# State-space recurrence by channel halves, and other PSUM banks for the input of the last experts

## The chip, the cores and the metric

The kernel runs on one core of one Trainium2 chip. The metric is the device time of a launch in microseconds (us). The core has five engines with a queue each: TensorE (PE in the profile; its weight loads are PEld), VectorE (DVE), ScalarE (ACT), GpSimd (POOL) and SyncE (SP), which here only issues DMAs. Each queue is worked off in order.

## What is computed

The model is a two-layer block on 64 x 32 tokens of width 256, and each sublayer adds its result to `x`. The order is: cross-attention, RWKV and a two-of-eight expert layer (layer 0); then cross-attention with quantised projections, a selective state-space model and a gated expert layer (layer 1). The change lies in the last two. Cut to what matters:

```python
# L1_attn: 512 inner channels, 16 states, over the 32 time steps of each sequence
xz = x @ in_proj_w.T + in_proj_b ; x_main, z = split(xz)
xc = silu(conv(x_main))
B, C, delta = split(xc @ x_proj_w.T + x_proj_b) ; dt = softplus(delta)
A = -exp(A_log)                                   # (512, 16)
h[t] = exp(A * dt[t]) * h[t-1] + dt[t] * B[t] * xc[t]     # for every channel and state
y[t] = sum_over_states(h[t] * C[t]) + D * xc[t]
out = layernorm(y * silu(z) @ out_proj_w.T + out_proj_b + x)
# L1_ffn: all eight experts are computed
g = softmax(2 * rmsnorm(x @ gate_w.T + gate_b)).max()
out = g' * sum_over_e( gelu(x @ w1[e] + b1[e]) @ w2[e] + b2[e] ),  g' = g / (g + 1e-6)
```

Ahead of each sublayer `x` is normalised over its 256 columns.

## The kernel before

The 2048 tokens are cut into four blocks of 512 (`BT`), numbered b = 0 to 3. In channel layout a block is a tile of 128 partitions (channels) by 512 columns (tokens), so the 512 inner channels are four such pieces, c = 0 to 3 (`C = 4`), and the 16 states are `N = 16`. `_stage3` is the quantised attention, `_stage4` the state-space model, `_stage5` the last experts. `layers` calls them interleaved: while attention works on the units of one block, the state-space model runs for the block before, and the experts for the one before that.

Stage 4 has three parts. `ahead(b)` normalises, projects in, convolves, and computes `dt` (its last step is L1077). `gates(v)` makes `zs = silu(z)`. `recur(b, v)` first makes `dtx = dt * xc` (L1096), sets `dt` to a huge value at the first step of each sequence so that the state starts anew (L1098, POOL), and then loops over the states n, and inside over the two halves of the channels, c2 = 0 and 2. A turn for one state and one half consists of

- L1105, POOL: `g = dtx * B`, 128 x 1024
- L1109, ACT: `h = exp(A * dt)` into a PSUM tile of the pool `psh` (tag "h", two banks), once for each of the half's two pieces
- L1110, DVE: the scan over time, in place, and L1111, DVE: `hc = h * C`, once for each piece
- L1116, POOL: `y += hc`, 128 x 1024 (`y` lies in the tile `xc`, by which name the profile knows it).

A recurrence is thus 32 turns and 64 tiles `h`. `B` and `C` of a state reach all partitions by one DMA of 512 KB from DRAM into a tile `bc` (L1102, SP queue), which serves both halves. `bc`, `g` and `hc` have two buffers each, in the last recurrence (b = 3, where memory of the attention has become free) three. After all states L1119 (POOL) multiplies each half of `y` by `zs`. Then come the output projection `outps` (L1131; L1156 in `end` for block 3), also in `psh`, and the layer norm.

Stage 5 has `head(b)` and `block(b)`. `head` normalises x (in the tile `xn5`, one buffer), transposes it through PSUM (`t_ps`, L1210, two tiles) into `xT`, copied by ACT (L1211), and computes the gate's logits (`lg_ps`, L1215) and the gate `gt`. `t_ps` and `lg_ps` lie in `psh` too. `block` streams eight experts' weights by two DMAs of 512 KB each (L1255 and L1256, SP queue), and for each of 32 pieces of the hidden layer does `up` (L1260, PE), a copy with bias (L1262, ACT), after four of them a Gelu (L1264, ACT), and `acc` (L1268, PE). The results are transposed (`rT`, L1281) and written out (L1284). `up` uses the pool `psu` (one bank); blocks 2 and 3 use attention's pool `ps` (two banks) for two of three pieces; `rT` is in `psu` for block 0 and in `ps` after it.

Nobody writes the order on an engine by hand. A planner works through the program with costs of its own: of what is ready on an engine, the earliest in program order goes first; a tile gets a bank or buffer of its tag when an earlier tile has given one back. The queues it makes are then fixed. The program order around the change is the end of `layers`: `s5(0)`, `head(1)`, `ahead(3)`, `recur(2)`, `gates(3)`, `head(2)`, `s5(1)`, `recur(3)`, `head(3)`, `s5(2)`, `s5(3)`, where `s5` is `block`.

Of the kernel before, what the change touches and what calls it, by code (L numbers as in the profile page):

```python
# [8 lines left out]
F32 = mybir.dt.float32  # L9
# [6 lines left out]
P = 128  # L16
# [3 lines left out]
NBLK = 4  # L20
BT = NTOK // NBLK
# [49 lines left out]
def _chan(k, name, j=0):  # L71
    at = CHAN_AT[name] + j
    return k.chan[:, at : at + 1]
# [40 lines left out]
def _norm(k, out, x, mv, rstd, j):  # L114
    k.nc.vector.tensor_scalar(out, x, mv[:, j, 0:1], rstd[:, j : j + 1], ALU.subtract, ALU.mult)
# [862 lines left out]
def _stage4(k, w, wk):  # L978
# [4 lines left out]
    nc, i = k.nc, k.i  # L983
    N, C = 16, 4
# [23 lines left out]
    def ph(shape, name):  # L1008
        return k.psh.tile(shape, F32, name=name, tag="h")
# [77 lines left out]
    def recur(b, v, mem=None):  # L1087
        xs = [k.x[b][:, j, :] for j in range(4)]
        dt, y = v.dt, v.y
        if b == NBLK - 1:  # L1090
            xn = residual(v, xs)
        own, more = (mem, 1) if mem else (wk, 0)
        dtx = wk.tile([P, C, BT], F32, name="dtx", tag="dtx", bufs=1)
        for c2, eng in ((0, nc.vector), (2, nc.gpsimd)):
            yc = y[:, c2 : c2 + 2]
            eng.tensor_tensor(dtx[:, c2 : c2 + 2], yc, dt.unsqueeze(1).to_broadcast([P, 2, BT]), ALU.mult)  # L1096

        nc.gpsimd.memset(dt.rearrange("p (b t) -> p b t", t=T)[:, :, 0:1], 1e20)  # L1098
        bc_rows = v.rows[0 : 2 * N].rearrange("(two n) t -> n two t", two=2)
        for n in range(N):  # L1100
            bc = own.tile([P, 2, BT], F32, name="bc", tag="bc", bufs=2 + more)
            nc.sync.dma_start(bc, bc_rows[n].partition_broadcast(P))  # L1102
            for c2 in range(0, C, 2):
                g = own.tile([P, 2, BT], F32, name="g", tag="g", bufs=2 + more)
                nc.gpsimd.tensor_tensor(g, dtx[:, c2 : c2 + 2], bc[:, 0:1, :].to_broadcast([P, 2, BT]), ALU.mult)  # L1105
                hc = own.tile([P, 2, BT], F32, name="hc", tag="hc", bufs=2 + more)
                for c in range(2):
                    h = ph([P, BT], "h")
                    nc.scalar.activation(h, dt, AF.Exp, scale=A[:, c2 + c, n : n + 1])  # L1109
                    nc.vector.tensor_tensor_scan(h, h, g[:, c, :], 0.0, ALU.mult, ALU.add)  # L1110
                    nc.vector.tensor_tensor(hc[:, c, :], h, bc[:, 1, :], ALU.mult)  # L1111
                if n == 0:

                    for c in range(c2, c2 + 2):
                        nc.scalar.activation(y[:, c, :], y[:, c, :], AF.Copy, scale=_chan(k, "L1_attn_D", c))
                nc.gpsimd.tensor_tensor(y[:, c2 : c2 + 2], y[:, c2 : c2 + 2], hc, ALU.add)  # L1116

        for c2 in range(0, C, 2):
            nc.gpsimd.tensor_tensor(y[:, c2 : c2 + 2], y[:, c2 : c2 + 2], v.zs[:, c2 : c2 + 2], ALU.mult)  # L1119
        if b == NBLK - 1:  # L1120
            for j2 in range(0, 4, 2):
                end(v, xs, xn, j2)
            return
        xn = wk.tile([P, 4, D], F32, name="xe4", tag="hc", bufs=2)
        xn = [xn[:, j, :] for j in range(4)]
        for j in range(4):
            nc.scalar.activation(xn[j], xs[j], AF.Identity, bias=v.off[:, j : j + 1], scale=v.rstd[:, j : j + 1])
            nc.gpsimd.tensor_tensor(xn[j], xn[j], bout, ALU.add)
            ps = ph([P, D], "outps")
            for c in range(C):  # L1130
                nc.tensor.matmul(ps, y[:, c, j * P : (j + 1) * P], wout[:, c, :], start=c == 0, stop=c == C - 1)  # L1131
            nc.vector.tensor_tensor(xn[j], ps, xn[j], ALU.add)
        mv, rstd = _stats(k, xn, "4b")
        for j in range(4):
            _norm(k, xn[j], xn[j], mv, rstd, j)
            nc.gpsimd.tensor_tensor(xn[j], xn[j], gamma, ALU.mult)
            nc.gpsimd.tensor_tensor(xs[j], xs[j], beta, ALU.add)
            nc.gpsimd.tensor_tensor(xs[j], xs[j], xn[j], ALU.add)

    def residual(v, xs):  # L1140


        xn = wk.tile([P, 4, D], F32, name="xr4", tag="xT4", bufs=1)
        for j in range(4):
            _norm(k, xn[:, j, :], xs[j], v.mv, v.rstd, j)
            nc.gpsimd.tensor_tensor(xn[:, j, :], xn[:, j, :], bout, ALU.add)
            nc.gpsimd.tensor_tensor(xs[j], xs[j], beta, ALU.add)
        return xn

    def end(v, xs, xn, j2):  # L1150

        ps = ph([P, 2, D], "outps")
        for j in range(2):
            for c in range(C):
                at = slice((j2 + j) * P, (j2 + j + 1) * P)
                nc.tensor.matmul(ps[:, j, :], v.y[:, c, at], wout[:, c, :], start=c == 0, stop=c == C - 1)  # L1156
        t = xn[:, j2 : j2 + 2, :]
        nc.vector.tensor_tensor(t, ps, t, ALU.add)
        mv, rstd = _stats(k, [t[:, j, :] for j in range(2)], "4e", wk, nc.vector)
        for j in range(2):  # L1160
            x = xs[j2 + j]
            nc.vector.scalar_tensor_tensor(t[:, j, :], t[:, j, :], mv[:, j, 0:1], gamma, ALU.subtract, ALU.mult)
            nc.vector.scalar_tensor_tensor(x, t[:, j, :], rstd[:, j : j + 1], x, ALU.mult, ALU.add)
# [7 lines left out]
def _stage5(k, w, out):  # L1171


    nc, i = k.nc, k.i
    E, H = 8, 4
# [8 lines left out]
    def ps(shape, name, free=False):  # L1184

        return k.ps.tile(shape, F32, name=name, tag="s") if free else k.psu.tile(shape, F32, name=name, tag="u")
# [6 lines left out]

    def head(b, mem):

        v = Ctx()
        xs = v.xs = [k.x[b][:, j, :] for j in range(4)]
        pairs = b == NBLK - 1
        if not pairs:
            mv, rstd = _stats(k, xs, "5")  # L1200
        xT = v.xT = mem.tile([P, 2, BT], F32, name="xT5", tag="xT5")
        for j2 in range(0, 4, 2):
            xn = k.wk5.tile([P, 2, D], F32, name="xn5", tag="xn5", bufs=1)
            t_ps = k.psh.tile([P, 2, 2 * P], F32, name="t_ps", tag="h")
            if pairs:
                mv, rstd = _stats(k, xs[j2 : j2 + 2], "5e", k.wk5, nc.vector)
            for j in range(2):
                _norm(k, xn[:, j, :], xs[j2 + j], mv, rstd, j if pairs else j2 + j)
                for c in range(2):
                    nc.tensor.transpose(t_ps[:, c, j * P : (j + 1) * P], xn[:, j, c * P : (c + 1) * P], k.ident)  # L1210
            nc.scalar.copy(xT[:, :, j2 * P : (j2 + 2) * P], t_ps)  # L1211
        lg_ps = k.psh.tile([P, 4, E], F32, name="lg_ps", tag="h")
        for j in range(4):
            for c in range(2):
                nc.tensor.matmul(lg_ps[:, j, :], xT[:, c, j * P : (j + 1) * P], wg[:, c, :], start=c == 0, stop=c == 1)  # L1215

        def rows(name):
            return k.small.tile([P, 4], F32, name=name, tag=name)

        def over(t):  # L1220
            return t.unsqueeze(2).to_broadcast([P, 4, E])

        lg = k.small.tile([P, 4, E], F32, name="lg", tag="lg", bufs=1)
        sq = k.small.tile([P, 4, E], F32, name="sq", tag="sq", bufs=1)
        nc.vector.tensor_tensor(lg, lg_ps, bg.unsqueeze(1).to_broadcast([P, 4, E]), ALU.add)
        nc.vector.tensor_tensor(sq, lg, lg, ALU.mult)
        ms, mx, gt, gn = rows("ms"), rows("mx"), rows("gt"), rows("gn")
        nc.vector.tensor_reduce(ms, sq, AX.X, ALU.add)
        _rsqrt(k, ms, [(ms, 1.0 / E, F32_EPS)], "5r")
        nc.vector.tensor_tensor(lg, lg, over(ms), ALU.mult)  # L1230
        nc.vector.tensor_tensor(lg, lg, rms.unsqueeze(1).to_broadcast([P, 4, E]), ALU.mult)
        nc.vector.tensor_reduce(mx, lg, AX.X, ALU.max)
        nc.vector.tensor_tensor(lg, lg, over(mx), ALU.subtract)


        nc.scalar.activation(lg, lg, AF.Exp, scale=2.0)
        nc.vector.tensor_reduce(gt, lg, AX.X, ALU.add)
        nc.vector.reciprocal(gt, gt)
        nc.vector.tensor_scalar(gn, gt, 1e-6, None, ALU.add)
        nc.vector.reciprocal(gn, gn)  # L1240
        nc.vector.tensor_tensor(gt, gt, gn, ALU.mult)
        v.gt = gt
        return v
# [213 lines left out]
```

## Time and profile before

| | us |
|---|---|
| median of 3 runs | 2025.51 (2022.17 to 2026.44) |
| profiled execution, time | 2021.33 |
| its span, first to last instruction | 2019.5 |
| POOL busy | 1107.0 (55%) |
| DVE busy | 1279.0 (63%) |
| ACT busy | 997.7 (49%) |
| first and last `h` of the four recurrences (ACT) | 780 to 999, 1102 to 1331, 1427 to 1662, 1715 to 1867 |
| first `up` and end of `acc` of the four expert blocks (PE) | 1109 to 1425, 1436 to 1727, 1717 to 1870, 1900 to 2013 |
| last attention softmax (ACT L893) | 1542 |

A row of a timeline has the start in us, the duration, the engine, the line, the operation, what it writes and reads, and in brackets how long the engine was idle before it and whose end released it. A row of the table by stretches has the length of the stretch and then the busy time of each engine, the granted clock of TensorE, the mean busy share of the DMA engines and what they moved in GB/s. Parts of one execution fit together to a hundredth of a microsecond; executions differ by more, as the range of the three runs shows.

### The profile page before, as it was taken

Reading aid. Unit: us, or ns where it says so; the run is one execution under the profiler, and the core shown is the slowest. Engines: PE = TensorE matmul, PEld = TensorE weight load, DVE = VectorE, ACT = ScalarE, POOL = GpSimd, SP = SyncE. Lnnn points to the kernel's source line nnn. Section 1 sums busy time; section 2 is a strip of 40 time slices with the busy share of each in tenths; the row PEclk is TensorE's granted clock in tenths of the full one; section 3 lists DMA queues with packets and bytes.
Section 4 is the critical chain, followed back from the end, with each engine's and each line's share of the span. In section 5 each row is a group of like instructions: output and inputs, shape, how many; then the busy total and the mean of one; then the engine's idle time right before and its main releaser. Section 6 shows DMA issues by size and latency. Waiting matters only on the chain. (4 is left out here: it accounts for less than half of the span.)

```text
span 2019.5 us, 20188 instructions
## 1 busy us (share of the span) xinstructions
PE 1563.2 (77%) x6323; PEld 805.4 (40%) x6323; DVE 1279.0 (63%) x2207; ACT 997.7 (49%) x2171; POOL 1107.0 (55%) x1369
## 2 busy tenths in 40 slices
PE   4775956849988978766778778779888575898798
PEld 3333523525645533433444334334443223333443
DVE  4578576376385267989854788763687593777300
ACT  3453453122554446445537567548466472676232
POOL 5444665423134225777853677763477777899100
PEclk9676877868998989767787889789888797898799
DMA  6755324020100202212201223202122130443021
GB/s 227 232 166 158 117 82 136 27 90 1 37 6 22 63 1 59 63 53 63 73 11 49 63 63 102 76 21 91 53 63 79 51 106 3 112 117 102 32 83 42
DMA packets 88379, 151.26 MB, mean 75 GB/s; under 512 B 7740, under 2 KB 52300, under 8 KB 86224
## 3 DMA queue, kind: packets, MB, share of 16 engines
q1 hardware_dynamic: 85428, 148.75, 24.2%
q10 hardware_dynamic: 2844, 1.22, 0.3%
q8 instruction: 50, 0.82, 0.2%
q14 instruction: 57, 0.47, 0.1%
HBM read 139.03 MB, written 10.92 MB: 74 GB/s over the span
## 5 line engine op out<-in xcount | busy, mean ns | idle before, releaser
L1105 POOL TENSOR_TENSOR g<-dtx,bc 128x1024 f32<-128x1024 f32 x128 | 301.9, 2362 | 126.3 <-DVE h L1110 89.0
L1110 DVE TENSOR_TENSOR_SCAN h<-h,g 128x512 f32<-128x512 f32 x256 | 307.5, 1218 | 62.3 <-ACT h L1109 59.4
L1116 POOL TENSOR_TENSOR xc<-xc,hc 128x1024 f32<-128x1024 f32 x128 | 303.6, 2374 | 23.9 <-DVE hc L1111 18.3
L1260 PE MATMUL up<-xT,w 128*128 128x512 f32 x512 | 274.4, 656 | 22.1 <-ACT hid L1262 21.7
L1268 PE MATMUL acc<-hid,w 128*128 128x512 f32 x512 | 266.5, 646 | 27.8 <-ACT hid L1264 27.8
L1109 ACT ACTIVATE h<-dt,A 128x512 f32<-128x512 f32 x256 | 173.6, 692 | 116.7 <-DVE hc L1111 116.0
L1111 DVE TENSOR_TENSOR hc<-h,bc 128x512 f32<-128x512 f32 x256 | 169.9, 679 | 3.9 <-DVE h L1110 0.4
L893 ACT ACTIVATE p<-sc,nm 128x256 f32<-128x256 f32 x256 | 117.7, 472 | 109.0 <-DVE nm L889 98.1
L1268 PEld LDWEIGHTS acc<-hid,w 128*128 128x128 f32 x512 | 101.8, 208 | 151.5 <-issue 108.4
L630 PE MATMUL weps<-we,xT 128*128 128x512 f32 x256 | 143.2, 687 | 17.5 <-DVE x L632 14.4
L1260 PEld LDWEIGHTS up<-xT,w 128*128 128x128 f32 x512 | 99.6, 207 | 134.6 <-issue 94.4
L1262 ACT ACTIVATE hid<-up,chan 128x512 f32<-128x512 f32 x128 | 86.5, 683 | 104.6 <-PE up L1260 104.4
L882 PE MATMUL sc<-kT,qm 32*128 32x256 f32 x512 | 115.4, 447 | 6.4 <-ACT p L893 2.4
L911 PE MATMUL pt_ps<-ident,p 128*128 128x128 f32 x512 | 90.3, 309 | 28.1 <-ACT p L893 28.0
L887 DVE TENSOR_REDUCE nm<-sc 128x2 f32<-128x512 f32 x128 | 84.1, 683 | 32.6 <-PE sc L882 31.6
L913 ACT COPY pt<-pt_ps 128x512 f32<-128x512 f32 x128 | 73.1, 587 | 46.5 <-PE pt_ps L911 37.7
L911 PEld LDWEIGHTS pt_ps<-ident,p 128*128 128x128 f32 x512 | 63.6, 155 | 69.0 <-ACT p L893 44.3
L247 POOL TENSOR_TENSOR cT<-cT,scb 128x2056 f32<-128x2056 f32 x16 | 74.4, 4648 | 27.4 <-PE sc L258 10.5
L530 POOL TENSOR_TENSOR kk<-kk 128x512 f32<-128x512 f32 x32 | 34.2, 1074 | 94.8 <-ACT kk L529 94.8
L919 PE MATMUL oT_ps<-pt,v 128*32 128x128 f32 x1024 | 68.4, 299 | 22.2 <-ACT pt L913 21.6
L882 PEld LDWEIGHTS sc<-kT,qm 32*128 32x128 f32 x512 | 67.5, 205 | 44.9 <-issue 17.8
L630 PEld LDWEIGHTS weps<-we,xT 128*128 128x128 f32 x256 | 50.6, 215 | 70.0 <-issue 51.9
(407 smaller groups left out, 3068.2 us busy)
## 6 DMA issues: line engine op xcount, KB each, us to landing
bc<-rows SPq DMA_DIRECT2D x64, 512.0 KB
w<-in_L_ffn_w_dram SPq DMA_DIRECT2D x64, 512.0 KB
cT<-in_ctxT_dram SPq DMA_DIRECT2D x16, 1028.0 KB
cq<-cq SPq DMA_DIRECT2D x32, 514.0 KB
cn<-in_ctx_dram SPq DMA_DIRECT2D x64, 256.0 KB
scb<-scales SPq DMA_DIRECT2D x16, 514.0 KB
kb<-steps SPq DMA_DIRECT2D x16, 514.0 KB
x<-in_x_dram SPq DMA_DIRECT2D x4, 512.0 KB
```

Of the source, the lines that this page charges most:

```text
L630: nc.tensor.matmul(ps, xT[:, c, r], we[:, c, e : e + 2, :], start=c == 0, stop=c == 1)
L882: nc.tensor.matmul(sc[h][:, f, :], qm[r, e + f].rearrange("p l n g -> p (l n g)"), kTs[e][r, f, :], start=True, stop=True,)
L893: nc.scalar.activation(w_[:, f, h - h0, :], sc[h][:, f, :], AF.Exp, bias=nm[:, e + f, h : h + 1], accum_out=sm[:, e + f, h : h + 1],)
L911: nc.tensor.transpose(pt_ps[:, h, m, :], ws[e, hp][:, f, h, m * P : (m + 1) * P], k.ident)
L1105: nc.gpsimd.tensor_tensor(g, dtx[:, c2 : c2 + 2], bc[:, 0:1, :].to_broadcast([P, 2, BT]), ALU.mult)
L1109: nc.scalar.activation(h, dt, AF.Exp, scale=A[:, c2 + c, n : n + 1])
L1110: nc.vector.tensor_tensor_scan(h, h, g[:, c, :], 0.0, ALU.mult, ALU.add)
L1111: nc.vector.tensor_tensor(hc[:, c, :], h, bc[:, 1, :], ALU.mult)
L1116: nc.gpsimd.tensor_tensor(y[:, c2 : c2 + 2], y[:, c2 : c2 + 2], hc, ALU.add)
L1260: nc.tensor.matmul(u, w1[e][:, c, q * P : (q + 1) * P], xT[:, c, :], start=c == 0, stop=c == 1)
L1262: nc.scalar.activation(hid[e][:, q, :], u, AF.Identity, bias=b1)
L1268: nc.tensor.matmul(acc[o], w2[e][:, q, o * P : (o + 1) * P], hid[e][:, q, :], start=n == H, stop=n == E * H + H - 1)
```

## The change

The loops of the recurrence are exchanged: first all 16 states of channels c = 0 and 1, then all 16 of c = 2 and 3. The load of `bc` moves with the inner loop, so each is made twice: 32 loads of 512 KB for a recurrence in place of 16. The product with `zs` follows each half directly.

In `head`, `t_ps` and `lg_ps` leave `psh` for blocks 0 to 2: blocks 0 and 1 take `psu` (one bank, shared with `up` and with `rT` of block 0), block 2 takes `ps` (two banks, attention's). Block 3 stays in `psh`.

```diff
         bc_rows = v.rows[0 : 2 * N].rearrange("(two n) t -> n two t", two=2)
-        for n in range(N):
-            bc = own.tile([P, 2, BT], F32, name="bc", tag="bc", bufs=2 + more)
-            nc.sync.dma_start(bc, bc_rows[n].partition_broadcast(P))
-            for c2 in range(0, C, 2):
+        for c2 in range(0, C, 2):
+            for n in range(N):
+                bc = own.tile([P, 2, BT], F32, name="bc", tag="bc", bufs=2 + more)
+                nc.sync.dma_start(bc, bc_rows[n].partition_broadcast(P))
                 g = own.tile([P, 2, BT], F32, name="g", tag="g", bufs=2 + more)
...
                 nc.gpsimd.tensor_tensor(y[:, c2 : c2 + 2], y[:, c2 : c2 + 2], hc, ALU.add)
 
-        for c2 in range(0, C, 2):
             nc.gpsimd.tensor_tensor(y[:, c2 : c2 + 2], y[:, c2 : c2 + 2], v.zs[:, c2 : c2 + 2], ALU.mult)
...
     def head(b, mem):
 
+
         v = Ctx()
+
+        def new(shape, name):
+            return k.psh.tile(shape, F32, name=name, tag="h") if b == NBLK - 1 else ps(shape, name, b >= 2)
+
...
-            t_ps = k.psh.tile([P, 2, 2 * P], F32, name="t_ps", tag="h")
+            t_ps = new([P, 2, 2 * P], "t_ps")
...
-        lg_ps = k.psh.tile([P, 4, E], F32, name="lg_ps", tag="h")
+        lg_ps = new([P, 4, E], "lg_ps")
```

## The prediction, made before the changed kernel ran

> **What bounds the kernel now.** I read the page first, then the busy time by stretches for the end, then the timelines of single engines where a recurrence begins, then the SP queue. The stretches, from the last attention units to the end:
>
> ```profile
> core 0: us, PE busy (x) PEld busy (x) DVE busy (x) ACT busy (x) POOL busy (x), PEclk, DMA share, GB/s
> 1383.00:1427.00 44.00, 41.73 (x200) 21.59 (x201) 17.18 (x34) 32.85 (x72) 9.30 (x7) 0.96 0.18 61
> 1427.00:1540.00 113.00, 91.35 (x441) 46.29 (x442) 87.03 (x132) 70.97 (x158) 78.59 (x78) 0.82 0.25 70
> 1540.00:1665.00 125.00, 91.30 (x237) 36.34 (x235) 93.20 (x112) 71.86 (x103) 94.57 (x85) 0.86 0.26 79
> 1665.00:1715.00 50.00, 28.41 (x81) 17.09 (x82) 16.08 (x36) 12.44 (x19) 38.42 (x60) 0.73 0.00 0
> 1715.00:1870.00 155.00, 132.30 (x287) 56.18 (x286) 120.21 (x144) 103.57 (x128) 143.12 (x75) 0.91 0.40 109
> 1870.00:1900.00 30.00, 15.27 (x65) 12.94 (x65) 16.42 (x90) 1.86 (x3) 5.40 (x3) 0.71 0.11 36
> 1900.00:2019.00 119.00, 113.53 (x265) 49.85 (x265) 3.96 (x16) 39.81 (x44) 2.76 (x14) 0.99 0.19 58
> ```
>
> The last 119 us are TensorE alone: block 3's experts, which need recurrence 3. That one (1715 to 1870) is POOL's: 143 of 155 us. In 1665 to 1715 no engine but POOL is half busy, and in 1383 to 1427 POOL works 9 of 44 us. Recurrences 3 and 2 begin where these two stretches end. Block 3's beginning, on ACT:
>
> ```profile
> 1698.17 0.69 ACT L1085 ACTIVATE zs<-inps,chan 128x512 f32<-128x512 f32 x1 [1.21 <-PE inps L1020]
> 1710.82 0.59 ACT L1211 COPY xT<-t_ps 128x512 f32<-128x512 f32 x1 [11.96 <-PE t_ps L1210]
> 1712.75 0.58 ACT L1211 COPY xT<-t_ps 128x512 f32<-128x512 f32 x1 [1.34 <-PE t_ps L1210]
> 1714.65 0.69 ACT L1109 ACTIVATE h<-dt,A 128x512 f32<-128x512 f32 x1
> ```
>
> POOL had made three tiles g for it, and dt was set, long before:
>
> ```profile
> 1669.23 0.12 POOL L1098 MEMSET dt<- 128x16 f32 x1
> 1669.31 6.95 POOL L1105 TENSOR_TENSOR g<-dtx,bc 128x1024 f32<-128x1024 f32 x3
> ```
>
> So the first h had its inputs at 1669.35. The two banks of psh were free from about 1691.5 (the last outps of block 2 is read at 1691.0 for 0.42 us), ACT idled 11.96 us, and still h came only after head(2)'s two copies: head(2) precedes recur(3) in the program, and its tiles come first in the bank's turn. Block 2 is the same with head(1), by two ACT rows and two of POOL:
>
> ```profile
> 1411.91 1.07 ACT L1211 COPY xT<-t_ps 128x512 f32<-128x512 f32 x2
> 1426.99 0.72 ACT L1109 ACTIVATE h<-dt,A 128x512 f32<-128x512 f32 x1
> 1387.01 4.71 POOL L1105 TENSOR_TENSOR g<-dtx,bc 128x1024 f32<-128x1024 f32 x2
> 1432.27 0.19 POOL L85 TENSOR_SCALAR rs_v<-ms 128x4 f32<-128x4 f32 x1 [31.59 <-DVE ms L1228]
> ```
>
> Its g were there at 1389.4; the first h came 37.6 us later, with POOL idle 31.59 us at one piece.
>
> **The change, part by part.** *Banks, recurrence 2.* Without t_ps and lg_ps in psh, the first h can run when g is ready: 1390 in place of 1427, 37 us earlier. From first h to last product hc it takes 1668.2 - 1427.0 = 241 us, 7.5 us a turn; its POOL work is 2 x 2.36 = 4.7, the rest is waiting among attention's work.
>
> *Banks, recurrence 3.* Three things must be ready for its first h: recurrence 2's outps read; dt; the banks. Recurrence 2's last product would fall at 1390 + 241 = 1631, and with the loads below at 1644; outps were given back 23 us after it (1668.2 to 1691.4), so at 1667. The other is ahead(3), which ends the attention's chain (last softmax 1542) and set dt at 1669.3. The earlier recurrence 2 puts work between attention's instructions from 1387 on; between 0 and 13 us for that (the POOL, DVE and ACT gaps it fills had been 35, 27 and 11 us, and attention stands earlier in the program), I take 9: first h at 1678 in place of 1714.65.
>
> *Banks, head(1).* Its three tiles now queue in psu behind block 0's last rT (PE, 1434.5) and before s5(1)'s first up (1435.9). Each needs PE, then ACT or DVE, some 5 us among other work: 15 us, bounds 5 and 40 (head(1) took 1382 to 1429 in psh). s5(1) waits for it. It has 16 us at a single bank's pace to regain: in 1665 to 1715 PE idles 21.6 us that no longer stand still, so s5(1) and s5(2) end 15 - 22 = 7 us earlier than 1870.0, at 1863. head(2) in ps finds both banks empty, since attention is over: nothing. head(0) has no up before it: nothing.
>
> *Loads.* 64 more DMAs of 512 KB. Bandwidth is no issue: in 1715 to 1870, 109 GB/s at a share of 0.40 becomes some 163 at 0.6. The wait is: a buffer bc is free after hc, then SP issues, then POOL may make g. Nearest rows, SP's issue and the g that waited for it:
>
> ```profile
> 1521.82 0.36 SPq L1102 DMA_DIRECT2D bc<-rows  x1
> 1527.70 2.37 POOL L1105 TENSOR_TENSOR g<-dtx,bc 128x1024 f32<-128x1024 f32 x1 [2.06 <-DMA bc<-rows]
> SPq L1102 <- DVE hc L1111: 515.1, 53, 27.2
> ```
>
> That is 5.9 us beside a weight load; another pair (1613.35 to 1618.42) is 5.1. I take 5.1. (The last line says that SP already stands 515 us at these loads until hc gives a buffer back.) A turn then loops through load 5.1, g 2.36, two scans 2 x 1.22, two products 2 x 0.68 and some 0.3 of handing over: 11.5 us per buffer. Two buffers give 5.8 us a turn, three 3.8. The Trainium skill (DMA: Bandwidth & Descriptors, "Anatomy of one DMA") has for a DMA 2.0 us fixed and bytes over 436 GB/s, given for GpSimd's queue: 3.2 us here. By it the loop is 9.6 us, two buffers give 4.8, as fast as POOL's 4.7, and the doubled loads cost nothing. The row is of this queue and has the wait's real end, so 5.8 decides.
>
> With two buffers (recurrences 0 to 2): the present turn of 7.5 exceeds 5.8, so the cost is 0 if the waits of a turn fall into the load's time; if all 2.8 us of them (7.5 - 4.7) come on top, 8.6. I take 7.9: 32 x 0.4 = 13 us each. Recurrences 0 and 1 hide it: recurrence 0 ends at 999 and the next starts at 1102, 1 ends at 1331 and the next has g at 1389. In recurrence 2 it is counted above.
>
> With three (recurrence 3): now 154.9 us from first h to last product (1714.65 to 1869.6), 4.84 a turn. Loop time 3.8 leaves 1 us a turn. Against it: at each Gelu DVE stands 2.5 us for h, and the lead of g, which covers that now, shrinks; and the bc loads queue in SP behind weight loads that wait for their own buffer (33.1 us in seven waits in 1715 to 1870, the longest 10.1). Bounds 0 and 29 (two-buffer pace 5.75); nearer to the first, since the loop fits: 12.
>
> *Product with zs.* The first half's leaves the tail, where it stands between two adds (L1119 at 1868.39, 2.35 us); POOL does it in mid-loop instead, zs being ready. Tail 1 us shorter. The first outps matmuls could start then; in before they held both banks for 13.6 us (1669.35 to 1682.94) waiting for the second half. If they took one during the second half, h would have one bank (0.69 + 1.22 + 0.68 + handing over, 2.9 a tile, 5.8 a turn): 16 us a recurrence. I take 0, because outps stand after all h in the bank's turn, as h stood behind t_ps above.
>
> **Sum,** in the profiled execution: first h 1678; last product 1678 + 154.9 + 12 = 1844.9; then 30.5 us (1869.6 to the first up of block 3 at 1900.1) less 1: 1874.4, later than 1863, so PE is free. Block 3 takes 119.4 us to the end: span 1993.8, with 1.8 outside it (2021.3 - 2019.5) 1995.6. The median shown is 1.0021 times the profiled run: 2000.
>
> **Rivals.** (1) *Full gain.* dt at 1669 as now and no cost of loads in recurrence 3: last product 1825, first up possible at 1855, but PE is busy to 1863: 1863 + 119.4 + 1.8, times 1.0021: 1988; if s5(2) also speeds up, 1978. For it: loop 3.8 under 4.7. Against: ahead(3) shares all engines with recurrence 2.
> (2) *Loads take the wait's place* (the slow side). In recurrence 3 the third buffer doesn't help, because weight loads hold SP: 5.75 and half of SP's 33 us on top, 6.3 a turn, 47 us more; recurrence 2 at 8.6 shifts the first h to 1687. First up 1687 + 154.9 + 47 + 29.5 = 1918: span 2038, time 2044. It decides from a turn of about 6.0 us (with 1678) on. For it: SP's 515 us. Against: w loads and bc loads alternate without delay now.
> (3) *psu becomes the bound.* head(1) takes 40 us: s5(2) ends at 1888, span 2007, time 2013.
> (4) *The waits were others'*: h waits for ACT's or DVE's attention work anyway, nothing gained, loads hidden: 2025.
>
> **How the numbers follow.** Forecast 0.46; (1) 0.15; (2) 0.26; (3) 0.07; (4) 0.06. A measurement of this kernel can tell about 0.2% from no change, 4 us: faster 0.67 (forecast, 1, 3 but for a part), same 0.07, slower 0.26. Range 1975 to 2045, from (1) to (2); the likeliest case's own is 1985 to 2015.
>
> **What would show it.** First h of blocks 2 and 3 near 1390 and 1678, ahead of the xT copies (if they follow them, the bank was not the wait). Turns of 7.9 and 5.2 us; POOL's g waiting for "DMA bc" (9.4 us in all now). The first up of block 1 near 1451; of block 3 near 1874 right after logits, with PE idle before it. I am wrong if POOL in recurrence 3 idles over 40 us on bc, or outps hold a bank inside a recurrence.

## The result, and the profile after

The changed kernel takes 2056.44 us (median of 4 runs, 2052.92 to 2057.84), the kernel before beside it 2023.84: the ratio is 1.0159, 95% interval 1.0138 to 1.0180. It is slower by 1.6%, where the forecast was 2000 us and the range ended at 2045. The profiled execution has a span of 2054.9 us, 35.4 more than before.

The busy time by stretches in the changed kernel, cut where its own stages begin (recurrence 2's first h, the last softmax, dt of block 3, the third turn of recurrence 3, its last product, block 3's first `up`):

```profile
core 0: us, PE busy (x) PEld busy (x) DVE busy (x) ACT busy (x) POOL busy (x), PEclk, DMA share, GB/s
1418.50:1582.80 164.30, 123.31 (x581) 64.65 (x582) 117.22 (x178) 94.88 (x226) 103.08 (x92) 0.76 0.33 90
1582.80:1704.90 122.10, 85.47 (x232) 38.69 (x231) 83.43 (x110) 63.32 (x88) 88.67 (x88) 0.86 0.35 93
1704.90:1748.40 43.50, 22.63 (x54) 10.58 (x53) 23.05 (x40) 23.20 (x28) 36.02 (x66) 0.78 0.15 49
1748.40:1891.70 143.30, 124.11 (x272) 52.97 (x271) 108.98 (x124) 95.55 (x118) 132.05 (x57) 0.93 0.61 162
1891.70:1927.20 35.50, 31.93 (x103) 18.33 (x103) 17.08 (x98) 10.54 (x13) 7.44 (x16) 0.95 0.11 32
1927.20:2054.90 127.70, 120.60 (x289) 52.90 (x287) 3.50 (x8) 42.22 (x46) 0.00 (x0) 1.00 0.22 70
```

Two things are new. The stretch of 30 us ahead of block 3's experts, in which PE had been half idle, now has PE busy for 31.9 of 35.5 us: it is still at block 2's experts. And a thin stretch has come back in another place, 1705 to 1748, at the start of recurrence 3, where of the main engines only POOL is over 60% busy.

What POOL and DVE wait for has changed too. Two groups of the page, first of the kernel before, then of the changed one (after the bar: idle time before the group and what ended most of it):

```profile
L1105 POOL TENSOR_TENSOR g<-dtx,bc 128x1024 f32<-128x1024 f32 x128 | 301.9, 2362 | 126.3 <-DVE h L1110 89.0
L1110 DVE TENSOR_TENSOR_SCAN h<-h,g 128x512 f32<-128x512 f32 x256 | 307.5, 1218 | 62.3 <-ACT h L1109 59.4
```

```profile
L1105 POOL TENSOR_TENSOR g<-dtx,bc 128x1024 f32<-128x1024 f32 x128 | 301.4, 2359 | 103.0 <-DMA bc<-rows 100.6
L1110 DVE TENSOR_TENSOR_SCAN h<-h,g 128x512 f32<-128x512 f32 x256 | 308.5, 1221 | 141.7 <-POOL g L1105 98.2
```

The instructions take the same time. But g had waited for DVE to give its own buffer back, and now waits 100.6 us for the load of bc (9.4 before), and DVE's scan waits 98.2 us for g. After 780 us, where the first recurrence begins, only one other wait for a DMA is seen in the trace (ACT, 3.7 us for dt's rows): the attention's own loads, which stand in the same SP queue, made no engine wait.

The banks did what the change says. POOL's setting of dt and ACT's first h, for recurrences 2 and 3, in the changed kernel:

```profile
1416.46 0.13 POOL L1098 MEMSET dt<- 128x16 f32 x1 [1.20 <-DVE dtx L1096]
1418.51 0.69 ACT L1109 ACTIVATE h<-dt,A 128x512 f32<-128x512 f32 x1
1704.91 0.13 POOL L1098 MEMSET dt<- 128x16 f32 x1
1708.15 1.30 ACT L1109 ACTIVATE h<-dt,A 128x512 f32<-128x512 f32 x2
```

The first h stands 2.0 and 3.2 us behind dt, where it had stood 40.1 and 45.4. It is dt that is late: 29.5 us for block 2 and 35.7 for block 3 against before, because attention is late (its last softmax ends at 1583 in place of 1542). The loads of bc lie in the chain of work that ended last. It runs back to 416 us and holds 14 loads of bc, of 4.6 to 7.4 us each, 73.8 us in all (the chain traced in the kernel before reaches back to 1614 us only, so there is no figure to set beside this). What such a wait does to attention is seen here, in four rows of the changed kernel (SP had issued this load at 1467.11):

```profile
1472.72 2.35 POOL L1105 TENSOR_TENSOR g<-dtx,bc 128x1024 f32<-128x1024 f32 x1 [3.18 <-DMA bc<-rows]
1475.10 1.23 DVE L1110 TENSOR_TENSOR_SCAN h<-h,g 128x512 f32<-128x512 f32 x1 [3.23 <-POOL g L1105]
1476.24 0.33 DVE L925 SCALAR_TENSOR_TENSOR od<-oT_ps,half,od 128x128 f32<-128x128 f32 x1
1476.62 0.59 PE L859 MATMUL kT_ps<-cq,b_L_xattn_wkvT 128*128 128x512 bf16 x2 [2.08 <-DVE od L925]
```

POOL waits for the load, DVE's scan for g, and behind the scan stands od, a step of the attention whose inputs were ready at 1473.5, 2.7 us earlier. PE's next product for the attention, kT_ps, waits for od in turn.

### The profile page after: what moved, and what is told of

Its sections match the earlier page's. It is cut to its first block, busy times and chain, and to the rows that moved or that the text cites. A ratio compares the mean times of both kernels' runs of the same rounds, so it can differ in the third digit from the quotient of the medians.

```text
span 2054.9 us, 20301 instructions
## 1 busy us (share of the span) xinstructions
PE 1579.9 (77%) x6323; PEld 814.3 (40%) x6323; DVE 1273.3 (62%) x2207; ACT 1005.3 (49%) x2175; POOL 1107.5 (54%) x1369
## 4 chain that ended last, share of the span: by engine, by line
PE 24%; POOL 21%; DVE 16%; issue 7%; ACT 7%; DMA 4%; SPq 0%; POOLq 0%; ACTq 0%; DVEq 0%
POOL xc L1116 6%; POOL g L1105 6%; PE up L1264 4%; PE acc L1272 4%; DVE h L1110 4%; DMA bc<-rows 4%; DVE hc L1111 2%; PE weps L630 2%; PE sc L882 2%; PE cv L539 2%; PE pt_ps L911 2%; DVE nm L887 1%; PE ck L527 1%; ACT p L893 1%; PE oT_ps L919 1%
## 5 line engine op out<-in xcount | busy, mean ns | idle before, releaser
L1110 DVE TENSOR_TENSOR_SCAN h<-h,g 128x512 f32<-128x512 f32 x256 | 308.5, 1221 | 141.7 <-POOL g L1105 98.2
L1105 POOL TENSOR_TENSOR g<-dtx,bc 128x1024 f32<-128x1024 f32 x128 | 301.4, 2359 | 103.0 <-DMA bc<-rows 100.6
L1264 PE MATMUL up<-xT,w 128*128 128x512 f32 x512 | 281.0, 671 | 36.0 <-ACT hid L1266 35.5
L1272 PE MATMUL acc<-hid,w 128*128 128x512 f32 x512 | 258.8, 628 | 24.2 <-ACT hid L1268 24.2
L911 PE MATMUL pt_ps<-ident,p 128*128 128x128 f32 x512 | 97.7, 330 | 34.0 <-ACT p L893 33.9
L911 PEld LDWEIGHTS pt_ps<-ident,p 128*128 128x128 f32 x512 | 69.7, 167 | 79.8 <-ACT p L893 52.2
L1020 PE MATMUL inps<-xT,w_L_attn_in_projT 128*128 128x512 f32 x128 | 72.8, 697 | 23.0 <-ACT zs L1085 16.9
```

The costliest lines, as they stand in the source:

```text
L911: nc.tensor.transpose(pt_ps[:, h, m, :], ws[e, hp][:, f, h, m * P : (m + 1) * P], k.ident)
L1264: nc.tensor.matmul(u, w1[e][:, c, q * P : (q + 1) * P], xT[:, c, :], start=c == 0, stop=c == 1)
L1272: nc.tensor.matmul(acc[o], w2[e][:, q, o * P : (o + 1) * P], hid[e][:, q, :], start=n == H, stop=n == E * H + H - 1)
```

## The experiments

Times in us from the span's start of each profiled execution; the ratio is that of the times to the kernel before on the same chip. "Turn" is the mean distance of the last products of recurrence 1, recurrence 2 and recurrence 3; "experts" is the first `up` of block 1, the end of `acc` of block 2, and the end of head(3)'s logits.

The expectations name three theories. L: the doubled loads cost the time (later split into L-buffer, the turn of the buffer, and L-traffic, the bytes themselves). P: the place of head(1) in the one bank of psu costs it. O: the new order of the loops costs it.

| kernel | ratio (95% interval) | last softmax | dt of blocks 2, 3 | turn | experts |
|---|---|---|---|---|---|
| before | 1 | 1542 | 1387, 1669 | 7.3, 7.5, 4.7 | 1436, 1870, 1900 |
| changed | 1.0159 (1.0138 to 1.0180) | 1583 | 1416, 1705 | 8.0, 8.5, 5.5 | 1490, 1937, 1920 |
| e1 banks alone | 0.9934 (0.9914 to 0.9953) | 1546 | 1395, 1665 | 7.6, 7.6, 5.0 | 1461, 1888, 1871 |
| e2 halves alone | 1.0191 (1.0148 to 1.0233) | 1566 | 1411, 1716 | 7.9, 8.0, 4.8 | 1476, 1919, 1935 |
| e3 old loops, two loads | 1.0212 (1.0168 to 1.0257) | 1575 | 1419, 1729 | 8.0, 8.2, 4.7 | 1484, 1930, 1947 |
| e4 change without reloads | 0.9892 (0.9843 to 0.9942) | 1543 | 1387, 1669 | 7.5, 7.4, 4.7 | 1455, 1879, 1861 |
| e5 change, bc split | 0.9958 (0.9943 to 0.9972) | 1562 | 1406, 1689 | 7.6, 7.4, 4.7 | 1475, 1899, 1881 |
| e6 old loops in 0 and 1 | 1.0052 (1.0031 to 1.0073) | 1560 | 1396, 1681 | 7.6, 8.4, 5.5 | 1467, 1911, 1894 |
| e7 block 2's banks alone | 0.9997 (0.9981 to 1.0012) | 1541 | 1386, 1669 | 7.4, 7.5, 5.6 | 1435, 1884, 1899 |
| e8 banks, block 1 in ps | 1.0202 (1.0176 to 1.0228) | 1537 | 1389, 1680 | 7.4, 7.3, 4.7 | 1591, 1943, 1867 |
| e9 banks, more up in ps | 1.0079 (1.0065 to 1.0094) | 1552 | 1399, 1678 | 7.6, 7.6, 5.0 | 1465, 1922, 1885 |
| e10 banks, bc split | 0.9885 (0.9862 to 0.9907) | 1543 | 1388, 1672 | 7.6, 7.4, 4.7 | 1456, 1879, 1861 |
| e11 halves, no reloads, old banks | 0.9939 (0.9917 to 0.9962) | 1535 | 1382, 1665 | 7.3, 7.7, 4.7 | 1429, 1862, 1892 |

**e1, the banks alone.** The edit is the second half of the change (`new` in `head`), with the loops as before.

> The banks of the change alone: head's tiles in psu or ps, the recurrence's loops as before, 16 loads of bc each. If the doubled loads are what costs (theory L), this is faster than before: first h of blocks 2 and 3 right behind the setting of dt, near 1390 and 1670 to 1680, attention's last softmax within 10 us of 1542, ratio to before 0.975 to 0.99. If the place of head(1) in the one bank psu is what costs (theory P: the first up of block 1 came 54 us later in the changed kernel), it is slower than before: block 1's first up 25 us late or more, ratio 1.005 or over.

It is faster than before, by 0.7% and not by 1 to 2.5%. Attention's end and dt are as expected. What is missing stands in the last column: block 1's experts begin 25 us late, block 2's end at 1888, 17 us after head(3) has its logits. PE does both until 1888, so of the 29 us by which the logits come earlier than before only 13 reach the end of the span. So theory L holds for the sign. What makes the experts late is in part the bank: head(0), which the prediction put at nothing, gets psu only behind another tile of that bank (its first transpose, at 1108.95, follows DVE's copy of the bias sums, L1192; before, it was at 1053.8), and block 0's experts end 7.6 us late; block 1's first up is 24.8 us late.

**e2, the loops alone.** The edit is the first half of the change.

> The loops of the change alone, head's tiles in psh as before. Theory L: turns of 7.9, 8.0 and 8.5 us as in the changed kernel, attention's end near 1583, and since the first h of blocks 2 and 3 wait for head's copies again, slower than the changed kernel, ratio to before 1.02 to 1.035. Theory P: block 1's first up no later than recurrence and attention make it, ratio 1.00 to 1.01, faster than the changed kernel.

The turns of recurrences 0 to 2 are 7.9, 7.9 and 8.0; the ratio lies just under the expected stretch. Attention ends at 1566, not at 1583: of the changed kernel's delay of 41 us the loops alone make 24, the banks alone (e1) 4, and the rest only the two together. The interval of the ratio and the changed kernel's overlap, so that e2 is slower than that one is not shown. Recurrence 3, with the same doubled loads and three buffers, has turns of 4.8 (4.7 before).

**e3, the doubled loads alone, in the old order.**

```diff
         for n in range(N):
-            bc = own.tile([P, 2, BT], F32, name="bc", tag="bc", bufs=2 + more)
-            nc.sync.dma_start(bc, bc_rows[n].partition_broadcast(P))
             for c2 in range(0, C, 2):
+                bc = own.tile([P, 2, BT], F32, name="bc", tag="bc", bufs=2 + more)
+                nc.sync.dma_start(bc, bc_rows[n].partition_broadcast(P))
```

> The kernel before, with one thing added: each turn loads its own bc, so 32 loads of 512 KB a recurrence with states outside and halves inside. Theory L: POOL's g waits for bc some 100 us in all and the turns are 7.9 to 8.5 us, as in the changed kernel, ratio to before 1.02 to 1.035. If instead the exchange of the loops is what costs (theory O: another order of the queues, the adds of one half after each other), it stays within 0.5% of before.

One DMA more for a state, and nothing else, costs 2.1%. The longest wait of POOL, by who was waited for (us in total, times, longest):

```profile
POOL g L1105 <- DMA bc<-rows: 115.0, 59, 4.5
```

59 waits of at most 4.5 us, a little less than a load. Theory O isn't needed: e3 has the old order and e2 the new one, both with 32 loads, and their intervals overlap.

**e4, the change without the reloads.**

```diff
+        bc = own.tile([P, 2, BT], F32, name="bc", tag="bc", bufs=2 + more)
+        nc.sync.dma_start(bc, bc_rows[0].partition_broadcast(P))
         for c2 in range(0, C, 2):
             for n in range(N):
-                bc = own.tile([P, 2, BT], F32, name="bc", tag="bc", bufs=2 + more)
-                nc.sync.dma_start(bc, bc_rows[n].partition_broadcast(P))
```

> The changed kernel, but bc is loaded once in a recurrence, for the first state, and all states use it (B and C of states 1 to 15 are left out, so y is another). This takes away the wait for the load and leaves order and banks. Theory L: no g waits for bc, turns of 7.0 to 7.5 us in recurrences 1 and 2 and 4.7 to 4.9 in 3, attention's end within 10 us of 1542, ratio to before 0.97 to 0.99. Theory O: attention's end stays near 1583 and the ratio over 1.005.

As theory L has it: no wait for bc, attention's end 1 us from before, 1.1% faster than before. The distance to the changed kernel is 1.0159 - 0.9892 = 2.7 points (per cent of the time before). But this run leaves out 31 of a recurrence's 32 loads, not only the 16 added ones. Against e1, which has the banks and 16 loads, the new loops cost 1.0159 - 0.9934 = 2.25 points.

**e5, the same bytes in two tiles.**

```diff
-                bc = own.tile([P, 2, BT], F32, name="bc", tag="bc", bufs=2 + more)
-                nc.sync.dma_start(bc, bc_rows[n].partition_broadcast(P))
+                bb = own.tile([P, BT], F32, name="bb", tag="bb", bufs=2 + more)
+                nc.sync.dma_start(bb, v.rows[n].partition_broadcast(P))
+                cc = own.tile([P, BT], F32, name="cc", tag="cc", bufs=2 + more)
+                nc.sync.dma_start(cc, v.rows[N + n].partition_broadcast(P))
```

> The changed kernel with bc split into a tile for B and one for C, each 256 KB, two buffers each (three in recurrence 3): the same bytes in twice as many DMAs and the same memory, but B's buffer is free again when g is made, not only after hc. If the wait comes from the turn of the buffers (load 5.1 us after the last hc, theory L-buffer), g's waits for the load fall from 100 us to under 40, turns of recurrences 0 to 2 to 7.0 to 7.6 us, attention's end to within 15 us of 1542, ratio to before 0.985 to 1.003. If it comes from the traffic itself (64 more loads on the DMA engines, theory L-traffic), waits and time stay as in the changed kernel, ratio 1.01 or over.

The waits for the loads are gone (POOL 0.9 us for B, DVE 2.0 for C) and the turns are back at 7.0, 7.6 and 7.4, with all of the bytes still moved, in more DMAs. So 1.0159 - 0.9958 = 2.0 of the 2.7 points go with the tile and not with the bytes: bc was held until the last hc, and the load could only then begin. The split also halves the load that g waits for, and no run separates that from the earlier release. The rest, 0.9958 against 0.9892, comes with an attention that ends 20 us later than in e4 (1562, not within 15 us of 1542 as expected) though hardly anybody waits for a load; whether that is the traffic, SP's queue or another order of the planner is open.

**e6, the old loops in recurrences 0 and 1.** `for n, c2 in order`, with the old order and one load a state if b < 2.

> The changed kernel with the old loops and 16 loads in recurrences 0 and 1, the new ones in 2 and 3. The prediction held that the slower turns of recurrences 0 and 1 are hidden: by that, this is no faster than the changed kernel, ratio to before 1.012 to 1.018. Theory L with queues (POOL and DVE stand for the load, and attention's work behind them in the queue stands with them): setting of dt of block 2 back near 1391 as with the banks alone (1413 in the changed kernel), and the last softmax within 25 us of 1546, ratio to before 0.997 to 1.007.

It is faster than the changed kernel by 1.07 points (some 22 us). dt of block 2 is back within 9 us of before, as in e1 (8). So the slower recurrences 0 and 1 were not hidden: they made up 1.07 of the 2.25 points between e1 and the changed kernel, nearly half.

**e7, of the banks only block 2's.** `ps(shape, name, True) if b == 2`, otherwise psh.

> The banks alone, and of them only block 2's (head(2) in ps); head(0) and head(1) stay in psh. In the run with all banks moved, block 1's experts began 25 us later than before (1460.7 in place of 1435.9) and block 3's waited for PE. If head(1)'s turn in psu is what ate the gain (theory P), block 1's first up returns to 1430 to 1440 and the ratio to before is 0.978 to 0.99; recurrence 2 then starts at 1425 again. If recurrence 2's earlier start is what the gain rests on, the ratio is 0.995 to 1.0.

Nothing is gained, and theory P fails in this form: block 1's first up is back at 1435 and the time doesn't follow. Recurrence 3's first h comes at 1689 in place of 1715, yet its last product at 1867.0 in place of 1869.6. The third turn of recurrence 3 begins at 1724.2, before at 1730.5: of the 25 us some 19 are lost in the first two turns (why, below), the others after them.

**e8, head(1) in attention's pool.** `ps(shape, name, True) if b in (1, 2)`.

> The banks alone, with head(1) in attention's pool ps as well as head(2); head(0) in psh. Recurrence 2 can then start at 1400 and head(1) need not wait for block 0's last experts. Theory P: block 1's first up at 1435 to 1445, ratio 0.975 to 0.988. Against: attention holds ps until 1542, three tiles more in its turn delay it by up to 10 us, then 0.99 to 1.0.

A miss on both sides. PE, when head(1) gets its banks, with block 1's first up in the last row:

```profile
1583.97 1.11 PE L1215 MATMUL t_ps<-ident,xn 128*128 128x128 f32 x4 [4.73 <-DVE x L798]
...
1591.05 1.20 PE L1265 MATMUL up<-xT,w 128*128 128x512 f32 x1
```

head(1) waits for attention's last use of ps (x of L798 is attention's very last write), so block 1's experts begin 155 us late. Recurrence 3 ends 30 us earlier than before (1839.3), and the program ends 42 us later in span (2061.6). The experts set the end here, not the recurrence.

**e9, more banks for block 1's experts.** `up` of block 1 uses ps for two of three pieces from n = 12 on, on top of e1.

> The banks alone, and from the 13th of block 1's 32 hidden pieces on, two of three up tiles go to attention's pool ps, as blocks 2 and 3 have it. With the banks alone, recurrence 3 ended 27 us earlier than before, and the experts of block 2 ended at 1888, after head(3)'s logits at 1871. If the experts' turn in the single bank psu is what now sets the end (theory P), block 1's acc ends some 15 to 30 us earlier than 1743, the first up of block 3 comes at 1855 to 1872 and the ratio to before is 0.98 to 0.99. If the recurrence sets the end, it stays at 0.993.

Also a miss, by the same rule: head(2)'s tiles stand before s5(1)'s in ps, and head(2) needs recurrence 2's result. Block 1's experts stood from 1594, the end of an `up`, until this:

```profile
1689.44 0.47 PE L1215 MATMUL t_ps<-ident,xn 128*128 128x128 f32 x1 [11.82 <-DVE xn L115]
...
1697.65 4.52 PE L1265 MATMUL up<-xT,w 128*128 128x512 f32 x6
```

Recurrence 3 ends 15 us earlier than before (1854.8), the program 20 us later: once more the experts' turn is what counts.

**e10, the banks with old loops and bc split.** The edit of e5 on top of e1.

> The banks alone, old loops with 16 loads, and bc split into a tile for B and one for C as in the run with the split tile. With the loop over halves the split brought 2.0%; here only 9.4 us of waits for bc are there to take in all, so theory L-buffer expects little: ratio to before 0.988 to 0.995. If more DMAs as such cost (the split run kept an attention end of 1562 without waiting), it is 0.995 to 1.003.

0.9885, at the lower end of what was expected: the fastest version that computes the whole model, ahead of both kernels (1.1% faster than before; 2.7% than the changed one, by the two ratios). It ties with e4. The waits for loads are gone in the old loops as well (9.1 us in e1), but that this is the reason isn't shown: most of the gain over e1 falls in recurrence 3, which takes 162.8 us in place of 175.1 and where g waited for no load in e1 either.

**e11, the halves without reloads, in the old banks.** The edit of e4 on e2.

> The loops of the change alone, bc loaded once in a recurrence (B and C of states 1 to 15 are left out), head's tiles in psh as before. This is the order by halves by itself, with neither reloads nor banks. Theory L: the order costs nothing, ratio to before 0.992 to 1.002, turns as before. Theory O: 1.005 or over.

By itself the order by halves shows no cost, as in e2 against e3. That it is 0.6% faster than before can't be put down to the order, since 15 of 16 loads are left out too.

## Why the prediction was wrong

**The banks, mechanism right.** "Without t_ps and lg_ps in psh, the first h can run when g is ready": it ran 2.0 and 3.2 us after dt. "The first outps matmuls ... I take 0": right too; no outps ran inside a recurrence.

**The length of a load, right.** Bandwidth: 163 GB/s at 0.6 was worked out, 162 at 0.61 is in the stretch of recurrence 3. Of the two figures for a load, the row's 5.1 us, which gives a loop of 5.8 a turn, and the estimate of 3.2 us from the Trainium skill (DMA: Bandwidth & Descriptors, "Anatomy of one DMA"), which gives a loop at no cost, the row's was the better: the loads in the chain above take 4.6 to 7.4 us, and with two buffers the loads cost 2.1% in e3.

**The cost of a turn, mis-sized.** I forecast turns of 7.9 us with two buffers, and they came out at 7.9, 8.0 and 8.5, but in part by luck: I had counted from 7.5, recurrence 2's turn, where recurrences 0 and 1 stood at 7.0 and 7.3. "I take 7.9: 32 x 0.4 = 13 us each" was about half of what recurrences 0 and 1 show: they became 26.8 and 22.1 us longer (26.3 and 22.2 in e2, the loops alone). Recurrence 2 became 29.7 us longer; in e2, where it starts later, 13.2. With three buffers I took 12 us. The last 30 turns of recurrence 3 take 143.3 us (4.8 each) where they took 139.1: 4 us, with 5.9 us of waits for bc. What I had named as a sign of being wrong, over 40 us of such waits in recurrence 3, would not have found the error: it lay in the recurrences before.

**Failed step 1: "Recurrences 0 and 1 hide it".** This put the cost of two recurrences at nothing. I counted the gap between a recurrence's end and the next one's beginning as slack. But that beginning is set by dt, and dt by attention, which runs on the same engines during the recurrence. With the doubled loads dt came 11 us later for block 1, 30 for block 2 and 36 for block 3; without reloads (e4) it didn't, with the old loops in recurrences 0 and 1 (e6) block 2's came only 9 late. Likewise I took 9, "between 0 and 13 us", for block 3's dt: it was 36. The way from the load to attention is the one of the rows above: g waits for bc, the scan for g, and attention's od stands behind the scan. The trace shows this for single loads; how many of attention's 41 us they make up is not shown.

**Failed step 2: the sum carried the first h's gain to the end.** I added recurrence 3's present length, 154.9 + 12, to its new first h. It took 183.5 us, 28.6 more than before: 24.4 in the first two turns and 4.2 in the other 30. DVE at its start, in the changed kernel:

```profile
1708.94 2.35 DVE L1110 TENSOR_TENSOR_SCAN h<-h,g 128x512 f32<-128x512 f32 x2 [4.96 <-ACT h L1109]
1715.90 2.27 DVE L115 TENSOR_SCALAR xe<-xe,mv,rstd 128x256 f32<-128x256 f32 x4 [4.61 <-POOL rstd L92]
...
1718.42 0.67 DVE L1111 TENSOR_TENSOR hc<-h,bc 128x512 f32<-128x512 f32 x1
...
1728.52 2.73 DVE L115 TENSOR_SCALAR xn<-x,mv,rstd 128x256 f32<-128x256 f32 x2 [3.73 <-POOL rstd L92]
...
1743.98 2.30 DVE L1234 TENSOR_TENSOR lg<-lg,ms 128x32 f32<-128x32 f32 x1 [3.94 <-POOL ms L92]
...
1748.41 2.35 DVE L1110 TENSOR_TENSOR_SCAN h<-h,g 128x512 f32<-128x512 f32 x2
```

The first scan is at 1708.9, and the loop runs from 1748.4. Between them DVE does recurrence 2's layer norm (L115 on xe), head(2)'s norm (xn) and its gate (lg), each at the end of a chain of small POOL instructions. They stand earlier in the program, and the queues hold them in order: the first hc had its scan done at 1711.3, yet DVE stood idle for 4.61 us until xe could run, and hc came behind it at 1718.4. I had read only who held the bank, and had put head(2) in ps at "nothing"; when the bank was free, the same work stood in the queue. e7, with block 2's banks alone and the old loads, shows the same: first h 25 us earlier, last product 2.6.

**Failed step 3: "later than 1863, so PE is free".** I gave head(1) 15 us in psu and let block 2's experts end at 1863. head(1) took some 20 us (block 0's last rT at 1469.5, the first up at 1490.2), and block 0's experts had themselves ended 31 us later. So block 2's ended at 1936.8. PE at the end, in the changed kernel, with head(3)'s logits finished at 1919.6:

```profile
1925.52 1.88 PE L1272 MATMUL acc<-hid,w 128*128 128x512 f32 x4
1927.24 1.88 PE L1264 MATMUL up<-xT,w 128*128 128x512 f32 x4
1929.69 7.13 PE L1272 MATMUL acc<-hid,w 128*128 128x512 f32 x16 [0.57 <-ACT hid L1268]
```

The up at 1927.24 is block 3's first, the acc after it block 2's last. So of the 35.4 us, 19.4 are head(3)'s logits (1919.6 against 1900.1), which come from recurrence 3; 7.8 are the wait behind block 2's experts up to 1927.2; and 8.2 are block 3's experts from there to the end (127.7 in place of 119.5), where PE still does block 2's last acc for 7.1 us, and its rT.

**The sum of the errors.** From the forecast span, 1993.8, to the measured one, 2054.9, are 61.1 us: 30.2 in the first h of recurrence 3 (1708.2 for 1678; step 1), 16.6 in its length (183.5 for 166.9; step 2), 6.1 from its last product to block 3's first up and 8.3 from there to the end (both step 3).

**The rivals.** The measured time lies beyond rival (2), "Loads take the wait's place", but for the most part not by its way. Its turn of 8.6 us in recurrence 2 came true (8.5); but it had put most of the cost, 47 us, into recurrence 3 with SP held by weight loads, and there the waits for bc are 5.9 us. Of rival (3), psu as the bound, the end came true and not the cause: PE is still at block 2's experts, but head(1) took 20 us and not 40; the whole chain of experts had begun later. I had the rivals as alternatives, and parts of both came together.

## What to carry to other kernels

A loop exchange that loads a tile twice has to be costed against the buffer's turn: load time plus the time until the last reader, divided by the buffers. That this lies under the mean turn is not enough: 5.8 under 7.0 to 7.5 cost 0.7 to 1.0 us a turn here, among attention's irregular waits, while 3.8 under 4.8, in a recurrence with little beside it, cost next to nothing. Splitting the tile by its readers, so that the first reader's part is free early, took back most of it. A gap between a stage's end and its next start is slack only if what sets the next start doesn't run on the same queues. And when a wait on a bank is removed, look at what else stands ahead in the queues of the engines concerned, and carry the gain along each chain to the end: here two chains, recurrence and experts, were within some 30 us of each other.

## What was not expected

Doubling one 512 KB load per state, 64 DMAs with 34 MB in all, cost 2.1% (e3) at a mean DMA share of about 30%; in recurrence 3 the same loads at a share of 0.61, with one buffer more, cost about 4 us in the changed kernel, and in e2 and e3 nothing that shows (155.4 and 153.1 us, 154.9 before). And e7 moved a recurrence's start, e8 a recurrence's end, by 25 to 30 us with no gain in time.
